# A graph layer on one core: destinations kept on chip and spread by TensorE, float32 queries, another order of loading

## The chip, the cores and the metric

The kernel runs on one core of a Trainium2 chip. The metric is the time of one execution on the device in microseconds (us), less is better; runs are repeated and the median is taken. The engines of the core are named as in the profile: PE (TensorE, matrix products; PEld is its loading of the stationary operand), DVE (VectorE), ACT (ScalarE), POOL (GpSimd, which here mostly issues indirect DMAs) and SP (SyncE, which here issues the plain DMAs). SBUF is the memory on chip with 128 partitions, PSUM the memory that PE writes its results to[...].

## The reference

There are 12500 nodes with 128 features each and 200000 edges, given by `src`, `dst` and `edge_weight`; the edges are sorted by `dst`. For each edge a score is computed from the query of its destination and the key of its source; every destination keeps its 16 best edges, takes a softmax over them, and adds up the messages of the sources. Cut to what matters:

```
h = maximum(layernorm(x), 0)
Qv = h @ W_Q.T ;  Ku = h @ W_K.T
score = sum(Qv[dst] * Ku[src]) / sqrt(128) * exp(-edge_weight)
keep  = rank of the edge among those of its dst, by score, is below 16
alpha = softmax over the kept edges of each dst
agg   = segment_sum(alpha * (h @ W_msg.T)[src], dst)
out   = x + relu(h @ W_self.T + agg)
```

## The kernel before

The edges are cut into chunks of 128, one edge to a partition, and 14 chunks make a group (`GC`); there are 112 groups (`G`). Because a destination's edges can run over the end of a group, a group looks at one chunk more, 15 in all (`NJ`). A group's destinations are at most 128 consecutive nodes, so that node rows also fit on the partitions. W_Q and W_K are multiplied into one matrix beforehand (`a_qk`), so that a query can be multiplied with the raw row `h[src]`.

A first part, the prologue, normalises x and writes h to a table in HBM (`h_tab`); turns the list of sources into columns (`idx_all`, L303 and the helper `to_columns`), and does the same with the destinations (`dst_all`), their places within a node (`pos_all`) and the decay (`dec_all`); and issues the gathers of the first seven groups on POOL, before the loop: the groups below `RAW` = 4 are read from x itself and normalised later (`raw_stats`, `raw_normed`), the others from `h_tab`. A gather (L172) is an indirect DMA of 128 rows of 512 bytes, one chunk; the rows of a group stand in a tile `hs`, of which there are seven.

The main loop (L684) is pipelined in software: iteration i works on different stages of groups i+4 to i-5, and the order of the instructions on each engine is written out by hand; nothing reorders them. In the order of the group's life the stages are:

- `load_nodes` (SP): the group's rows of h and of x. `load_dst` (SP, L186): its 1920 destination numbers, the same on all 128 partitions, 960 KB, into `dstb`.
- `let_go`, called by `more(k)`: DVE copies two columns of `idx_all` into a tile `ix` (L472), and POOL issues two gathers with it. So the place of `more(k)` in DVE's order paces the gathers. `more(0)` and `more(1)` come before `best`, `more(2)` right after it, `more(5)` is the first of the next group and takes a new `hs`.
- `h_turned` (PE L499), `h_turned_out` (ACT L503), `q_made` (PE L506) and `q_out` (ACT L510): the queries of the 128 nodes. `q_parts` (DVE L516) splits each query into three bf16 numbers that add up to it.
- `far_of` (ACT L522): for node p and edge e, the square of dst(e) minus the node's number, from `dstb` and a bias `nb`. `to_edges` (ACT L527): relu(1 - far), which is 1 where they are equal and 0 elsewhere. This is the 0/1 matrix `to_e`, in bf16.
- `q_to_edges` (PE L546), in four blocks of four chunks: the queries put on the edges, the 0/1 matrix times each of the three parts, added up in PSUM, bank "q".
- `scores` (DVE L556): the product with the gathered row, summed over the features, times the decay. `scores_in_slots` (DVE L564), `slots_by_node` (PE L569 and L571), `slots_out` (ACT L576), `node_by_slots` (PE L579): the scores of a node brought beside each other, 40 slots a node, bank "e".
- `best` (DVE L585 to L597): the 16 best of each node. `sum_of_exps` (ACT L602), `one_over_sum` (DVE).
- `kept_to_edges` (PE L614): what a node kept, back on the edges by the 0/1 matrix, bank "x". `on_edges` (DVE L620 to L627), `exps` (ACT L631), `weights` (DVE L635 and L636, into `alz`).
- `sums` (PE L646) in two halves: the weighted sums of the rows of `hs` by node, bank "a". When the second half is done the `hs` is free. `sums_out` (ACT L651), `sums_turned` (PE L654), `sums_turned_out` (ACT L658), `products` (PE L661 and L662), `output` (DVE L666), `store` (SP L672).

Two lines say how the index columns and the broadcast are moved:

```
nc.sync.dma_start(dstb[:, 0:hi - lo], dst[lo:hi].partition_broadcast(P))          # L186
nc.vector.tensor_copy(ix[:, j0:j1], idx_all[:, GC * g + j0:GC * g + j1])          # L472
```

Of the kernel before, what the change touches and what calls it, by code (L numbers as in the profile page):

```python
# [10 lines left out]
F32 = mybir.dt.float32  # L11
BF16 = mybir.dt.bfloat16
I32 = mybir.dt.int32
U32 = mybir.dt.uint32
AF = mybir.ActivationFunctionType
OP = mybir.AluOpType
# [4 lines left out]
P = 128  # L21
# [20 lines left out]
RAW = 4  # L42
# [18 lines left out]
def bc(ap, n):  # L61

    return ap.unsqueeze(2).to_broadcast([ap.shape[0], ap.shape[1], n])


def upper(ap):

    return ap.bitcast(BF16).rearrange("p (n two) -> p n two", two=2)[:, :, 1]


def bm(ap, n):

    return ap.unsqueeze(1).to_broadcast([ap.shape[0], n, ap.shape[1]])
# [3 lines left out]
def gnn_layer(  # L77
# [38 lines left out]
    CPR = 13  # L116
# [4 lines left out]
    assert RR <= P and RR - RF <= 1  # L121
# [10 lines left out]
    def bank(tag, bufs):  # L132
        return psum.tile([P, 512], F32, tag=tag, bufs=bufs, name=tag)
# [10 lines left out]
    nvec = const.tile([P, 1], F32, name="nvec")  # L144
    a_qk = const.tile([P, P], F32, name="a_qk")
# [8 lines left out]
    nb = const.tile([P, G], F32, name="nb")  # L154
# [21 lines left out]
    def gather_at_once(g, table):  # L176
        gather(g, 0, own[g], lambda j: idx_all[:, GC * g + j:GC * g + j + 1], table)

    def load_dst(g):
        n = chunks[g] * P  # L180
        lo = g * EG
        T[g]["dstb"] = dstb = rows_pool.tile([P, NJ * P], I32, name="dstb", bufs=2)
        hi = min(lo + n, M)
        if hi < lo + n:
            nc.vector.memset(dstb[:, hi - lo:n], 1 << 21)
        nc.sync.dma_start(dstb[:, 0:hi - lo], dst[lo:hi].partition_broadcast(P))  # L186
# [47 lines left out]
    with tc.tile_pool(name="edges", bufs=1) as ep, ExitStack() as stage:  # L234
        prep = stage.enter_context(tc.tile_pool(name="prep", bufs=1))
        RL = HALO + RW

        src_r = ep.tile([RR, RL], I32, name="src_r")
        h0 = src_r.bitcast(F32)
        h1 = alz[0][0:RR, 0:RL]  # L240
        dst_all = alz[1][:, 0:CW]
        assert max(RL, CW) <= NJ * (WW + STEP)
        dst_r = ep.tile([RR, HALO + RW], I32, name="dst_r")
# [6 lines left out]
        def load_rows(t, a):  # L250
            if RF:
                nc.scalar.dma_start(t[0:RF, 0:RW], a[0:RF * RW].rearrange("(p c) -> p c", c=RW))
            if REM:
                nc.scalar.dma_start(t[RF:RF + 1, 0:REM], a[RF * RW:M].rearrange("(p c) -> p c", p=1))
# [13 lines left out]
        nc.vector.memset(src_r, 0)  # L268
        load_rows(src_r, src)
        xs, t = [], 0  # L270
        for i, n in enumerate(sizes):
            xg = prep.tile([HP, n, D], F32, name=f"xg{i}")
            for a, b in cuts:
                nc.sync.dma_start(xg[a:b], by_part(x)[a:b, t:t + n, :])
            xs.append((t, n, xg))
            t += n
        make_identity(nc, ident)
        nc.gpsimd.iota(dst_r, pattern=[[1, RL]], base=1 << 21, channel_multiplier=0)
        nc.gpsimd.memset(dst_r[0:1, 0:HALO], -1)
        nc.gpsimd.iota(slots, pattern=[[1, KM]], base=0, channel_multiplier=0,  # L280
# [3 lines left out]
        nc.vector.memset(ew_r, 0.0)  # L284
# [10 lines left out]
        nc.vector.memset(dst_all[:, RR * CPR:CW], float(1 << 21))  # L295
# [13 lines left out]
        def finish(i):  # L309
            t0, n, xg = xs[i]  # L310
            normed(xg, n, *stat[i])
            if i == 1:
                for t, w in zip(ws, (w_q, w_k, w_self, w_msg)):
                    nc.scalar.dma_start(t, w)
                nc.scalar.dma_start(b_i[:, 1:G],
                                    bass.AP(dst.tensor, dst.offset + EG - 1, [[EG, 1], [EG, G - 1]]))

                nc.scalar.dma_start(dst_r[0:1, HALO:], dst[0:RW].rearrange("(p c) -> p c", p=1))
                if RF > 1:
                    nc.scalar.dma_start(dst_r[1:RF, :], bass.AP(dst.tensor, dst.offset + RW - HALO,  # L320
                                                                [[RW, RF - 1], [1, RL]]))
                if REM:
                    nc.scalar.dma_start(dst_r[RF:RF + 1, 0:HALO + REM],
                                        dst[RF * RW - HALO:M].rearrange("(p c) -> p c", p=1))
                load_rows(ew_r, ew)
            for a, b in cuts:
                nc.sync.dma_start(by_part(h_tab)[a:b, t0:t0 + n, :], xg[a:b])
            if i == 1:
                load_dst(0)
# [6 lines left out]
        for g in range(RAW, min(7, G)):  # L336
            gather_at_once(g, h_tab)
# [18 lines left out]
        nc.vector.tensor_copy(row_i[:, 1, G - TAIL:G], row[:, 3, 0:TAIL])  # L356
        pb = bank("s", 1)
# [5 lines left out]
        nc.vector.tensor_copy(dst_f, dst_r)  # L363
        nc.vector.memset(h0[:, 0:1], 0.0)
        nc.vector.tensor_tensor(h0[:, 1:RL], dst_f[:, 1:RL], dst_f[:, 0:RL - 1], op=OP.is_equal)
        nc.vector.tensor_tensor_scan(h1, h0, h0, 0.0, op0=OP.mult, op1=OP.add)
        bb = rows_pool.tile([P, 2, G], F32, name="bb")
        nc.vector.tensor_copy(bb, pb[:, 0:2 * G].rearrange("p (a g) -> p a g", a=2))
        nc.vector.tensor_scalar(nb, bb[:, 0, :], nvec, -1.0, op0=OP.add, op1=OP.mult)
        to_columns(dst_f, HALO, lambda at, p: nc.scalar.copy(at(dst_all), p))  # L370
        to_columns(h1, HALO, lambda at, p: nc.scalar.copy(at(pos_all), p))
        to_columns(ew_r, 0, lambda at, p: nc.scalar.activation(at(dec_all), p, AF.Exp, scale=-1.0))

        byg = dst_all.rearrange("e (g j) -> e g j", j=GC)
        nc.vector.tensor_sub(dlw[:, :, 0:GC], byg[:, 0:G, :], bc(bb[:, 0, :], GC))
        nc.vector.tensor_sub(dlw[:, :, GC], byg[:, 1:G + 1, 0], bb[:, 0, :])
        nc.vector.tensor_tensor(dlw, dlw, bm(w0, G), op=OP.subtract)
        for k in range(2):
            nc.vector.memset(alz[k], 0.0)
# [10 lines left out]
        nc.vector.tensor_copy(badc, bad)  # L390
        t0 = ep.tile([P, TAIL], F32, name="t0")
# [64 lines left out]
    with tc.tile_pool(name="win", bufs=2) as win:  # L456
# [7 lines left out]
        def let_go(g, k):  # L464

            j0, j1 = 2 * k, min(2 * k + 2, own[g])
            if j0 >= j1:
                return
            if k == 0:
                T[g]["ix"] = win.tile([P, GC], I32, name="ix", bufs=4)  # L470
            ix = T[g]["ix"]
            nc.vector.tensor_copy(ix[:, j0:j1], idx_all[:, GC * g + j0:GC * g + j1])  # L472
            gather(g, j0, j1, lambda j: ix[:, j:j + 1])

# [33 lines left out]
        def q_out(g):  # L508
            T[g]["q"] = win.tile([P, 3, D], F32, name="q", bufs=3)
            nc.scalar.copy(T[g]["q"][:, 0, :], so[:, P:2 * P])  # L510

        def q_parts(g):

            q = T[g]["q"]
            for k in range(2):
                nc.vector.tensor_sub(q[:, k + 1, :], q[:, k, :], upper(q[:, k, :]))  # L516


        def far_of(g):
            n = chunks[g] * P  # L520
            T[g]["far"] = win.tile([P, NJ * P], BF16, name="far", bufs=1)
            nc.scalar.activation(T[g]["far"][:, 0:n], T[g]["dstb"][:, 0:n], AF.Square, bias=nb[:, g:g + 1])  # L522

        def to_edges(g):
            n = chunks[g] * P
            T[g]["to_e"] = win.tile([P, NJ * P], BF16, name="to_e", bufs=4)
            nc.scalar.activation(T[g]["to_e"][:, 0:n], T[g]["far"][:, 0:n], AF.Relu, bias=1.0, scale=-1.0)  # L527
# [11 lines left out]
        def q_to_edges(g, b):  # L539
            j0, j1 = 4 * b, min(4 * b + 4, chunks[g])  # L540
            if j0 >= j1:
                return
            T[g]["pq", b] = pq = bank("q", 3)
            for j in range(j0, j1):
                for k in range(3):
                    nc.tensor.matmul(pq[:, (j - j0) * P:(j - j0 + 1) * P],  # L546
                                     lhsT=T[g]["to_e"][:, j * P:(j + 1) * P], rhs=upper(T[g]["q"][:, k, :]),
                                     start=(k == 0), stop=(k == 2))
# [62 lines left out]
        def kept_to_edges(g):  # L611
            T[g]["px"] = px = psum.tile([P, NJ + 1, 64], F32, tag="x", bufs=1, name="x")
            for j in range(chunks[g]):
                nc.tensor.matmul(px[:, j, 0:KM + 3], lhsT=T[g]["to_e"][:, j * P:(j + 1) * P],  # L614
                                 rhs=upper(T[g]["km"]), start=True, stop=True)
# [63 lines left out]
        def at(g, stage, *args):  # L679
            if 0 <= g < G:  # L680
                stage(g, *args)


        for i in range(-3, G + 6):  # L684
            at(i + 3, load_nodes)
            if i + 2 > 0:
                at(i + 2, load_dst)
# [7 lines left out]
            def more(k):  # L695

                g, k = (i + 3, k + 2) if k < 5 else (i + 4, k - 5)
                if 7 <= g < G:
                    let_go(g, k)

            at(i, q_to_edges, 0)
            at(i - 5, output)
# [3 lines left out]
            at(i - 4, sums_turned)  # L706
            at(i - 4, sums_turned_out)
            at(i + 1, q_out)
            at(i, q_to_edges, 1)
            at(i + 1, far_of)  # L710
            at(i - 1, slots_by_node)
            at(i + 1, places)
# [12 lines left out]
            at(i + 1, q_parts)  # L725
# [204 lines left out]
```

## Time and profile before

| | before |
|---|---|
| median of 10 runs | 2691.07 us (2688.03 to 2692.63) |
| profiled execution | 2693.51 us |
| its span, first to last instruction | 2691.7 us |
| granted TensorE clock, mean | 0.694 |
| PE / PEld busy | 1716.5 us (64%) / 1464.7 us (54%) |
| DVE busy | 1475.2 us (55%) |
| POOL busy | 1520.3 us (56%), 1578 instructions |
| ACT busy | 647.9 us (24%) |
| DMA | 253.17 MB, mean 94 GB/s |

How to read it: a profile is one execution. In the lists of groups, a line gives the kernel's line, the engine, the operation, the tiles written and read, their shape and type, and the count; then the busy time in us and the mean of one in ns; then the idle time of the engine just before these instructions and what ended most of it. "remote" is a semaphore whose giver the profile does not name, "issue" is time in which the engine waited for nothing that the profile shows. In the list of waits a line gives engine, tile, line, what it waited for, and then the total in us, how often, and the longest. In the timeline a line gives the start and the duration in us, and in brackets the idle time before. A float32 product has two records of PEld and two of PE, a bf16 product one of each.

### The profile page before, as it was taken

What the parts mean: (1) busy time and instruction counts of PE and PEld (TensorE: products, weight loads), DVE (VectorE), ACT (ScalarE), POOL (GpSimd) and SP (SyncE); (2) the same over time, 40 slices, a digit from 0 to 9 for tenths busy, and PEclk for the clock granted to TensorE, in tenths of its full rate; (3) what the DMA queues carried; (4) which work ended last, traced back from release to release, by engine and by line L of the source; (5) the groups of instructions that cost most, each with busy time, mean ns of one, the idle gap of its engine ahead of it and who ended that gap; (6) DMA issues with size and microseconds to landing.
All of it is one profiled execution on the core that took longest, in us unless ns stands there. A gap on an engine that the chain in (4) does not pass through costs nothing. (4 is left out here: it accounts for less than half of the span.)

```text
span 2691.7 us, 43581 instructions
## 1 busy us (share of the span) xinstructions
PE 1716.5 (64%) x14574; PEld 1464.7 (54%) x14575; DVE 1475.2 (55%) x7420; ACT 647.9 (24%) x1306; POOL 1520.3 (56%) x1578
## 2 busy tenths in 40 slices
PE   0226666766666666666666666666666666766666
PEld 0125555655555555555555555555556555655555
DVE  5446655555555555555555555555555555555555
ACT  5532222222222222222222222222222222222221
POOL 4725555555555555555555555555556555555550
PEclk9667776677677676676666766666676666666778
DMA  8412323232333323322232332322333333222320
GB/s 217 156 57 87 97 92 94 92 94 94 93 95 95 95 94 94 94 90 88 89 93 91 95 94 93 94 94 94 95 95 94 94 93 90 87 90 92 93 80 8
DMA packets 117572, 253.17 MB, mean 94 GB/s; under 512 B 32798, under 2 KB 76065, under 8 KB 116576
## 3 DMA queue, kind: packets, MB, share of 16 engines
q1 hardware_dynamic: 66104, 144.92, 15.6%
q0 software_dynamic: 50144, 102.74, 14.3%
q10 hardware_dynamic: 1094, 2.69, 0.5%
q8 instruction: 115, 1.88, 0.3%
q14 instruction: 115, 0.94, 0.1%
HBM read 236.40 MB, written 14.40 MB: 93 GB/s over the span
## 5 line engine op out<-in xcount | busy, mean ns | idle before, releaser
L172 POOL DMA_INDIRECT hs<-h_tab,ix x1465 | 1410.6, 963 | 1044.0 <-DVE prod L556 493.7
L546 PE MATMUL q<-q,to_e 128*128 128x128 bf16 x5022 | 553.8, 260 | 316.1 <-issue 261.8
L646 PE MATMUL a<-hs,alz 128*128 128x128 f32 x3348 | 694.3, 373 | 92.3 <-issue 81.0
L646 PEld LDWEIGHTS a<-hs,alz 128*128 128x128 f32 x3348 | 636.7, 279 | 140.4 <-issue 119.7
L546 PEld LDWEIGHTS <-to_e 128*128 128x128 bf16 x5022 | 421.8, 116 | 396.5 <-issue 384.6
L556 DVE SCALAR_TENSOR_TENSOR prod<-hs,dec_all,q 128x128 f32<-128x128 f32 x1674 | 483.0, 342 | 75.5 <-remote 35.4
L585 DVE TENSOR_SCALAR ell<-slots,e 128x40 f32<-128x40 f32 x112 | 28.0, 250 | 869.8 <-remote 811.2
L571 PE MATMUL e<-ow,sl 128*41 128x40 f32 x3348 | 251.2, 251 | 44.0 <-issue 42.1
L602 ACT ACTIVATE e<-v,km 128x16 f32<-128x16 f32 x112 | 34.4, 307 | 976.8 <-DVE km L594 959.7
L571 PEld LDWEIGHTS e<-ow,sl 128*41 128x41 f32 x3348 | 221.3, 166 | 68.7 <-issue 54.3
L654 PE MATMUL s<-ident,agn 128*128 128x128 f32 x112 | 41.2, 368 | 301.7 <-ACT up L631 153.9
L651 ACT ACTIVATE agn<-a,rden 128x128 f32<-128x128 f32 x112 | 41.1, 367 | 766.4 <-remote 515.2
L522 ACT ACTIVATE far<-dstb,nb 128x1920 bf16<-128x1920 int32 x112 | 213.0, 1902 | 0.0
L527 ACT ACTIVATE to_e<-far 128x1920 bf16<-128x1920 bf16 x112 | 201.1, 1796 | 0.0
L654 PEld LDWEIGHTS s<-ident,agn 128*128 128x128 f32 x112 | 17.7, 158 | 326.1 <-ACT up L631 172.2
L556 DVE DVE_READ_ACCUMULATOR prod<-hs,dec_all,q 128x1 f32 x1674 | 136.1, 81 | 0.0
L472 DVE COPY ix<-idx_all 128x2 int32<-128x2 int32 (+1 forms) x733 | 130.2, 178 | 0.0
L614 PE MATMUL x<-km,to_e 128*128 128x43 bf16 x1674 | 81.1, 203 | 42.8 <-DVE km L597 21.4
L614 PEld LDWEIGHTS <-to_e 128*128 128x128 bf16 x1674 | 67.9, 111 | 68.2 <-DVE km L597 44.0
L666 DVE SCALAR_TENSOR_TENSOR o<-s,x_t 128x128 f32<-128x128 f32 x112 | 32.5, 290 | 128.8 <-issue 119.3
L506 PE MATMUL s<-a_qk,hT 128*128 128x128 f32 x224 | 56.9, 337 | 64.5 <-ACT hT L503 55.9
L564 DVE TENSOR_TENSOR sl<-po,s 128x600 f32<-128x600 f32 x112 | 87.5, 782 | 4.4 <-DVE prod L556 0.6
(166 smaller groups left out, 1634.8 us busy)
## 6 DMA issues: line engine op xcount, KB each, us to landing
dstb<-in_dst_dram SPq DMA_DIRECT2D x111, 960.0 KB
hs<-h_tab,ix POOLq DMA_INDIRECT x1465
h_r<-h_tab SPq DMA_DIRECT2D x112, 64.0 KB
x_t<-in_x_dram SPq DMA_DIRECT2D x108, 64.0 KB
out_dram<-o SPq DMA_DIRECT2D x108, 64.0 KB
xg<-in_x_dram SPq DMA_DIRECT2D x2, 1400.0 KB
h_tab<-xg SPq DMA_DIRECT2D x2, 1400.0 KB
xg<-in_x_dram SPq DMA_DIRECT2D x1, 1120.0 KB
```

The costliest lines, as they stand in the source:

```text
L172: nc.gpsimd.indirect_dma_start(out=T[g]["hs"][:, j, :], out_offset=None, in_=table[0:N, :], in_offset=bass.IndirectOffsetOnAxis(ap=index(j ...
L472: nc.vector.tensor_copy(ix[:, j0:j1], idx_all[:, GC * g + j0:GC * g + j1])
L506: nc.tensor.matmul(so[:, P:2 * P], lhsT=T[g]["hT"], rhs=a_qk, start=True, stop=True)
L522: nc.scalar.activation(T[g]["far"][:, 0:n], T[g]["dstb"][:, 0:n], AF.Square, bias=nb[:, g:g + 1])
L527: nc.scalar.activation(T[g]["to_e"][:, 0:n], T[g]["far"][:, 0:n], AF.Relu, bias=1.0, scale=-1.0)
L546: nc.tensor.matmul(pq[:, (j - j0) * P:(j - j0 + 1) * P], lhsT=T[g]["to_e"][:, j * P:(j + 1) * P], rhs=upper(T[g]["q"][:, k, :]), start=(k ...
L556: nc.vector.scalar_tensor_tensor(prod, rows_of(g, j), dec_all[:, c:c + 1], T[g]["pq", b][:, (j % 4) * P:(j % 4 + 1) * P], op0=OP.mult, op1 ...
L564: nc.vector.tensor_tensor(sl1[g % 2][:, 0:n, 0:KM], T[g]["po"][:, 0:n, :], bc(T[g]["s"][:, 0:n], KM), op=OP.mult)
L571: nc.tensor.matmul(et[0:KM + 1, STEP * j:STEP * j + WN], lhsT=sl1[g % 2][:, j, :], rhs=T[g]["ow"][:, j, :], start=False, stop=(j == n - 1))
L614: nc.tensor.matmul(px[:, j, 0:KM + 3], lhsT=T[g]["to_e"][:, j * P:(j + 1) * P], rhs=upper(T[g]["km"]), start=True, stop=True)
L646: nc.tensor.matmul(T[g]["pa"][:, 0:P], lhsT=alz[g % 2][:, WW * j + PRE:WW * j + PRE + P], rhs=rows_of(g, j), start=(j == 0), stop=(j == n ...
L654: nc.tensor.transpose(so[:, 2 * P:3 * P], T[g]["agn"], ident)
```

## The change

The destination numbers are no longer loaded once more for each group as a broadcast. The rows of `dst_r`, which the prologue loads anyway, are kept on chip as `rel`, one group to a row: destination minus the number of the group's first node, in bf16, 1920 to a row. For group g, PE multiplies one column of the identity matrix, repeated 128 times, with `rel`, which puts row g on all partitions, in four pieces of up to 512 columns in PSUM. ACT squares each piece with the node's own number as a bias. The pieces use bank "a", which has one buffer and also holds the sums; a piece can be written when ACT has read the one before. Their places in the order of the loop are shown in the diff.

The 0/1 matrix is in float32 and so is q; `q_parts` is gone and `q_to_edges` has one float32 product for a chunk in place of three bf16 ones. `kept_to_edges` reads the upper halves of the float32 numbers as a strided bf16 operand.

In the prologue all loads are issued by SP, the sources first, where ACT issued some of them before. `RAW` is 3: 42 gathers are issued at once from x. The gathers of group 3 go through `let_go` between steps of the prologue on DVE, those of groups 4, 5 and 6 are issued in the iterations -1, 0 and 1 of the loop. A row of the prologue's tiles is now a whole group (`CPR` = `GC`), `dlw` is made from `rel` with matrix products, and the memset of `alz` is done by POOL.

```diff
-RAW = 4
+RAW = 3
...
-    CPR = 13
+    CPR = GC
...
+    rel = const.tile([RR, RW + P], BF16, name="rel")
...
-    def load_dst(g):
-        n = chunks[g] * P
-        lo = g * EG
-        T[g]["dstb"] = dstb = rows_pool.tile([P, NJ * P], I32, name="dstb", bufs=2)
...
-        nc.sync.dma_start(dstb[:, 0:hi - lo], dst[lo:hi].partition_broadcast(P))
+    def let_go(g, k):
+
+        j0, j1 = 2 * k, min(2 * k + 2, own[g])
+        if j0 >= j1:
+            return
+        if k == 0:
+            T[g]["ix"] = rows_pool.tile([P, GC], I32, name="ix", bufs=6)
+        ix = T[g]["ix"]
+        nc.vector.tensor_copy(ix[:, j0:j1], idx_all[:, GC * g + j0:GC * g + j1])
+        gather(g, j0, j1, lambda j: ix[:, j:j + 1])
...
-                nc.scalar.dma_start(t[0:RF, 0:RW], a[0:RF * RW].rearrange("(p c) -> p c", c=RW))
+            nc.sync.dma_start(t[0:RF, 0:RW], a[0:RF * RW].rearrange("(p c) -> p c", c=RW))
...
+        for k in range(2):
+            nc.gpsimd.memset(alz[k], 0.0)
...
-        for g in range(RAW, min(7, G)):
-            gather_at_once(g, h_tab)
...
+        let_go(RAW, 0)
...
+        nc.vector.tensor_scalar(rel, dst_f[:, HALO:], dst_f[:, HALO - 1:HALO], 1.0, op0=OP.subtract, op1=OP.subtract)
+        let_go(RAW, 2)
...
-            T[g]["q"] = win.tile([P, 3, D], F32, name="q", bufs=3)
-            nc.scalar.copy(T[g]["q"][:, 0, :], so[:, P:2 * P])
-
-        def q_parts(g):
-
-            q = T[g]["q"]
-            for k in range(2):
-                nc.vector.tensor_sub(q[:, k + 1, :], q[:, k, :], upper(q[:, k, :]))
-
-
-        def far_of(g):
-            n = chunks[g] * P
-            T[g]["far"] = win.tile([P, NJ * P], BF16, name="far", bufs=1)
-            nc.scalar.activation(T[g]["far"][:, 0:n], T[g]["dstb"][:, 0:n], AF.Square, bias=nb[:, g:g + 1])
+            T[g]["q"] = win.tile([P, D], F32, name="q", bufs=3)
+            nc.scalar.copy(T[g]["q"], so[:, P:2 * P])
+
+
+        def far_of(g, b):
+            n0, n1 = 4 * P * b, min(4 * P * (b + 1), chunks[g] * P)
+            if n0 >= n1:
+                return
+            if b == 0:
+                T[g]["far"] = win.tile([P, NJ * P], BF16, name="far")
+            pr = bank("a", 1)
+            nc.tensor.matmul(pr[:, 0:n1 - n0], lhsT=upper(ident[0:RR, g:g + 1]).to_broadcast([RR, P]),
+                             rhs=rel[:, n0:n1], start=True, stop=True)
+            nc.scalar.activation(T[g]["far"][:, n0:n1], pr[:, 0:n1 - n0], AF.Square, bias=minus)
...
-            T[g]["to_e"] = win.tile([P, NJ * P], BF16, name="to_e", bufs=4)
+            T[g]["to_e"] = win.tile([P, NJ * P], F32, name="to_e", bufs=4)
...
-                for k in range(3):
-                    nc.tensor.matmul(pq[:, (j - j0) * P:(j - j0 + 1) * P],
-                                     lhsT=T[g]["to_e"][:, j * P:(j + 1) * P], rhs=upper(T[g]["q"][:, k, :]),
-                                     start=(k == 0), stop=(k == 2))
+                nc.tensor.matmul(pq[:, (j - j0) * P:(j - j0 + 1) * P],
+                                 lhsT=T[g]["to_e"][:, j * P:(j + 1) * P], rhs=T[g]["q"], start=True, stop=True)
...
-                nc.tensor.matmul(px[:, j, 0:KM + 3], lhsT=T[g]["to_e"][:, j * P:(j + 1) * P],
+                nc.tensor.matmul(px[:, j, 0:KM + 3], lhsT=upper(T[g]["to_e"][:, j * P:(j + 1) * P]),
...
-            if i + 2 > 0:
-                at(i + 2, load_dst)
...
-                g, k = (i + 3, k + 2) if k < 5 else (i + 4, k - 5)
-                if 7 <= g < G:
+                if i in (-1, 0, 1):
+                    g = i + 5
+                else:
+                    g, k = (i + 3, k + 2) if k < 5 else (i + 4, k - 5)
+                    if g < 7:
+                        return
+                if i >= -1 and g < G:
                     let_go(g, k)
 
             at(i, q_to_edges, 0)
+            at(i + 1, far_of, 0)
             at(i - 5, output)
             at(i - 5, store)
             at(i - 3, weights)
             more(0)
             at(i - 4, sums_turned)
+            at(i + 1, far_of, 1)
             at(i - 4, sums_turned_out)
             at(i + 1, q_out)
             at(i, q_to_edges, 1)
-            at(i + 1, far_of)
+            at(i + 1, far_of, 2)
             at(i - 1, slots_by_node)
+            at(i + 1, far_of, 3)
             at(i + 1, places)
...
-            at(i + 1, q_parts)
```

## The prediction, made before the changed kernel ran

> **What bounds the kernel now.** I read the groups first, then the waits of 1000 to 2000 us, then the timeline of single cycles. The chain of what ended last covers only the last microseconds and says nothing of the loop. In the groups the reader should compare counts with idle time:
>
> ```profile
> L172 POOL DMA_INDIRECT hs<-h_tab,ix x1465 | 1410.6, 963 | 1044.0 <-DVE prod L556 493.7
> L546 PE MATMUL q<-q,to_e 128*128 128x128 bf16 x5022 | 553.8, 260 | 316.1 <-issue 261.8
> L646 PE MATMUL a<-hs,alz 128*128 128x128 f32 x3348 | 694.3, 373 | 92.3 <-issue 81.0
> ...
> L585 DVE TENSOR_SCALAR ell<-slots,e 128x40 f32<-128x40 f32 x112 | 28.0, 250 | 869.8 <-remote 811.2
> ...
> L522 ACT ACTIVATE far<-dstb,nb 128x1920 bf16<-128x1920 int32 x112 | 213.0, 1902 | 0.0
> ...
> dstb<-in_dst_dram SPq DMA_DIRECT2D x111, 960.0 KB
> ```
>
> No engine is full. POOL issues 1465 gathers in the loop, each 0.96 us busy and about 0.30 us of issue: 14 x 1.25 = 17.5 us a group. The loop from the first of them (215.4 us) to the last (2614.5) takes 2399 us for 105 groups, 22.85 us each, so about 5.3 us per cycle is POOL waiting. The waits say for what:
>
> ```profile
> DVE ell L585 <- remote: 353.6, 41, 8.7
> ...
> POOL hs L172 <- DVE prod L556: 187.6, 86, 4.3
> ```
>
> DVE stands 8.7 us a cycle before `best` (L585), and POOL once up to 4.3 us behind DVE, because the next index copy (L472) is queued behind `best`. One cycle in time:
>
> ```profile
> 1552.74 0.29 PE L571 MATMUL e<-ow,sl 128*41 128x40 f32 x3 [0.19 <-issue]
> ...
> 1555.60 0.99 PE L546 MATMUL q<-q,to_e 128*128 128x128 bf16 x5 [0.49 <-issue]
> ...
> 1557.33 0.94 POOL L172 DMA_INDIRECT hs<-h_tab,ix  x1 [0.30 <-issue]
> ...
> 1560.03 0.25 DVE L585 TENSOR_SCALAR ell<-slots,e 128x40 f32<-128x40 f32 x1 [8.74 <-remote]
> ...
> 1562.42 0.94 POOL L172 DMA_INDIRECT hs<-h_tab,ix  x1 [4.15 <-DVE prod L556]
> ```
>
> L585 waits for the last L571. PE's record of it ends at 1553.03, yet DVE starts 7 us later, 1.76 us after the last gather was issued (1558.27), when its packets had landed. Meanwhile PE makes a pass or a handful, waits 0.5 us for nothing the profile shows ("issue"), and goes on. **While gathers stream, PE crawls and what it has done reaches the others late.** Two more places support this. In the last iterations, without gathers, the same wait is nothing:
>
> ```profile
> 2624.79 0.25 DVE L585 TENSOR_SCALAR ell<-slots,e 128x40 f32<-128x40 f32 x1 [0.35 <-PE e L571]
> ```
>
> Those iterations last 12.5 to 14.3 us, though they too read a broadcast `dstb`. And in the prologue, where POOL issues gathers without a pause until 160.9 us, PE hardly moves from 118 on and then stands:
>
> ```profile
> 169.25 0.79 PE L506 MATMUL s<-a_qk,hT 128*128 128x128 f32 x2 [45.61 <-ACT hT L503]
> ```
>
> So a cycle is: eight gathers (10.0 us), a gap of 4.1 (drain 1.8, `best` 2.0, copy and issue 0.4), six gathers (7.5), a gap of 1.7 until the sums of L646 give an `hs` buffer back. Sum 23.3 less the 0.3 issue counted at each gap: 22.7, against 22.85.
>
> **Part by part, for one group in the loop.**
>
> *The 960 KB broadcast goes.* 111 x 960 KB is 43% of the 253 MB moved. No instruction waits for it in the listing of 1000 to 2000 us, L522 has 0.0 us idle before it, and SP only issues it. Its removal frees nothing on the path. Two bounds: if the broadcast slows the gathers' landing, the 1.8 us of drain could fall to 1 us (-0.8); but in the packets it holds the gathers back some 2 to 3 us at each cycle's start, in which PE works at its normal rate (L571's 27 passes in 1.81 us from 1550.74). Without it the crawl begins earlier: up to the 30 passes of L571, 1.4 us hot and 2.1 cold, move behind the drain (+1.4 to +2.1). I take the second, since the stall follows gathers in every stretch above.
>
> *Four products and four reads of PSUM replace L522.* Before: one ACT instruction of 1.90 us, from SBUF. After: for each of four pieces, PE (at most 512 columns, four bf16 passes' worth of 0.070, 0.28 us, twice that at half the clock) and ACT's Square. The nearest ACT row is the prologue's read of 128x484 from PSUM: four in 2.90 us, 0.73 each. So ACT 2.9 instead of 1.9 us (+1.0, ACT is busy 24%: hidden), PE +1.1 to +2.2. The new thing is the chain: all pieces use the one buffer of bank "a", so each product waits for ACT to have read the piece before, and the sums (L646), which share it, wait for the last. By the program's order pieces 0, 1 and 2 stand on PE ahead of L571; piece 3 stands behind it and ahead of q's third block, the transposition L499 and the first half of the sums. Queued behind a waiting piece is therefore all PE work of `best`, and behind that DVE's index copies, POOL's next six gathers.
> A hop from PE to ACT costs 0.96 us when the stream has not started (L654 1548.85, aggT 1549.81). Inside it the trace has one:
>
> ```profile
> 1643.54 0.45 PE L654 MATMUL s<-ident,agn 128*128 128x128 f32 x1 [6.54 <-issue]
> ...
> 1648.08 0.27 ACT L658 COPY aggT<-s 128x128 f32<-128x128 f32 x1 [10.97 <-remote]
> ```
>
> That is 4.5 us. Three hops of 1 us would fit into the ten of the burst (bound +0); if one of them ends only with the drain, piece 2 (0.3 to 0.5) and the passes of L571 (1.4 to 2.1) come after it, where now only 0.4 us does. Together with the lost lull, the same passes are late, once: **+1.8 us**, the range 0 to 2.5.
>
> *q in float32, one product.* Before 3 x 15 bf16 passes: 12 take 0.84 us hot, 0.070 each, 3.15 us. After 2 x 15 passes such as L646's, 16 in 2.00, 0.125 each: 3.75. The Trainium skill (FP8 and Floating Point Precision, TensorE Precision Notes) says that true FP32 takes four passes: 15 x 4 x 0.070 = 4.2 us, +1.05, which speaks against the change; the row has two longer records and +0.6. I take the row. Most lies beside DVE's scores; what falls between `best` and the release of `hs` counts, with piece 3 and its read ahead of the sums: block 2 and piece 3 add 0.2 + 0.4 + 0.75 = 1.3 us there, of which `best` itself (2.0 us on DVE) covers most: **+0.4 us** (0 to 1.3). If that cover is gone the scatter to the edges (L614) falls into the second burst, which is the second rival below. DVE loses L516, 2 x 0.3 = 0.6 us a group; it stands behind the index copies on DVE and DVE waits 8.7 us a cycle: nothing.
>
> *L614 reads every second bf16 of the float32 matrix.* No row shows a strided load; L614's 15 loads take 0.54 us, twice that would be +0.5, less than nothing is excluded since the count is the same. I take 0, keeping 0.5.
>
> *The prologue.* 42 gathers are issued from x at once, then those of group 3 between DVE steps and 14 in each of the windows -1, 0, 1; POOL issues the same 1563 in all. Before, POOL stands from 160.9 to 215.4 us, and the loop that started at 94 stood for the 98 gathers. After, group 3 can follow `h_tab` (about 108 us), three windows at a loop's pace with gathers, 22 us, end at 175, and two windows without (12.5 to 14) bring group 7 at about 200 or a little earlier. The memset of `alz` goes from DVE to POOL before the gathers. All loads on SP's queue, the sources ahead, can bring the first gather (24 us) forward by some us; the x loads and `h_tab` stores queued behind them on SP may lose as much. **-20 us**, between 0 and -40 (all of the stand but one window).
>
> *Sum.* 105 x (1.8 + 0.4) = +231; -20; profiled execution 2693.5, so 2904. The median of the runs shown is 2.4 below that execution: about **2900**.
>
> **Rivals.**
> *A, the cycle stays, only the prologue gains.* For it: the cycle is 22.8 to 22.9 us at a granted clock of 0.5 as at 1.0, so PE's own length doesn't show; the three hops fit if each takes 1 us. Against: the 4.5 us hop. 2691 - 20 = 2671, between 2650 and 2690.
> *B, the stall shrinks.* If it is DMA traffic as such, 43% less of it takes drain and part of the crawl away: cycle 21 us, 105 x -1.85 - 20 gives 2477, up to 2600. Against: iterations with `dstb` but no gathers show no stall.
> *C, both gaps grow.* In one cycle of before (1456.7 to 1484.5) L614 slipped into the second burst: `on_edges` came late, the second gap was 6.3 us instead of 1.7, the cycle 27.6. If piece 3 and the longer products do this each time: 105 x 4.75 - 20 = +479, 3170; half the cycles, 2930.
> *D, slower only by the prologue:* sources and nodes behind one queue, nothing in the loop: 2700 to 2715.
>
> **How the numbers follow.** Forecast, 2780 to 3030, 0.42. C above that, 0.17. A 0.21, B 0.15, D and no change 0.05. Faster by over 0.2% (about what a measurement here tells from no change) is A and B, 0.36; within it 0.03; slower 0.61. The range reaches from B's upper part to C's time, 2560 to 3180; the forecast's own is 2780 to 3030.
>
> **What would show it.** Right: the gap on POOL before the six gathers is 5.5 to 6.5 us and ends with L585's successor, the index copy; L571's counterpart lies after the burst; ACT's pieces of `far` are spread over the burst, one at least over 3 us behind its product; the iterations at the end without gathers are 13 to 16 us. Wrong: pieces following each other at 1 us inside the burst (A), the wait of `best` ending while gathers flow, or gathers closer than 1.25 us (B); a second gap over 4 us (C). The sum fails altogether if the crawl was due to the broadcast after all, or if the bursts are cut into other lengths than eight and six.

## The result, and the profile after

| | before | after |
|---|---|---|
| median | 2691.03 us (31 runs, 2683.88 to 2696.47) | 2660.69 us (9 runs, 2646.53 to 2667.04) |
| ratio | | 0.9884, interval 0.9871 to 0.9896 |
| span of the profiled execution | 2691.7 us | 2658.9 us |
| 99th gather (the first of group 7) | 215.4 us | 207.0 us |
| from there to the last gather | 2399.1 us | 2373.5 us |
| last gather to the end | 77.1 us | 78.4 us |
| DMA | 253.17 MB | 143.40 MB |
| granted TensorE clock, mean | 0.694 | 0.777 |

The change made the kernel 1.2% faster where 8% slower was forecast. The difference of the spans, 32.8 us, is 8.4 us before the loop's gathers and 25.6 us within them, less 1.3 us behind them. One thing must be known to read the rest: in the sets of runs below the kernel before took 2691, 2715 to 2717 or, in one set, 2081 us, so every ratio is to runs of the kernel before in the same set, on the same chip.

The groups of the page of the changed kernel that answer to those shown of before:

```profile
L174 POOL DMA_INDIRECT hs<-h_tab,ix x1521 | 1478.3, 972 | 1027.2 <-DVE prod L545 377.5
L635 PE MATMUL a<-hs,alz 128*128 128x128 f32 x3348 | 577.3, 341 | 443.9 <-ACT far L513 351.8
...
L536 PE MATMUL q<-q,to_e 128*128 128x128 f32 x3348 | 617.5, 332 | 84.7 <-issue 76.8
...
L513 ACT ACTIVATE far<-a,minus 128x512 bf16<-128x512 f32 (+1 forms) x447 | 294.9, 660 | 942.0 <-remote 648.8
...
L574 DVE TENSOR_SCALAR ell<-slots,e 128x40 f32<-128x40 f32 x112 | 28.1, 251 | 798.6 <-remote 756.6
```

And its waits of 1000 to 2000 us:

```profile
DVE ell L574 <- remote: 317.5, 41, 8.6
ACT far L513 <- remote: 263.1, 41, 7.3
...
PE a L635 <- ACT far L513: 161.2, 35, 5.6
POOL hs L174 <- DVE prod L545: 142.8, 42, 4.0
```

The picture of before is still there: `best` (now L574) waits 7.7 us each time it waits (317.5 in 41), POOL behind it. The new waits that the prediction spoke of are there too: ACT's piece waits 6.4 us each time, and the sums (L635) 4.6 us for ACT. Yet the cycle didn't grow. One cycle shows why:

```profile
1503.89 0.94 POOL L174 DMA_INDIRECT hs<-h_tab,ix  x1 [1.81 <-PE q L536]
...
1505.27 0.38 PE L511 MATMUL a<-rel,ident 112*128 112x512 bf16 x1 [0.66 <-ACT far L513]
...
1505.68 0.69 ACT L513 ACTIVATE far<-a,minus 128x512 bf16<-128x512 f32 x1 [0.47 <-issue]
...
1506.76 0.63 PE L511 MATMUL a<-rel,ident 112*128 112x512 bf16 x1
...
1507.43 0.69 ACT L513 ACTIVATE far<-a,minus 128x512 bf16<-128x512 f32 x1 [0.74 <-PE a L511]
1507.57 2.14 PE L560 MATMUL e<-ow,sl 128*41 128x40 f32 x30
...
1509.64 0.34 PE L511 MATMUL a<-rel,ident 112*128 112x384 bf16 x1
...
1509.81 1.05 PE L536 MATMUL q<-q,to_e 128*128 128x128 f32 x8
...
1512.83 0.94 POOL L174 DMA_INDIRECT hs<-h_tab,ix  x1 [0.31 <-issue]
...
1515.39 0.25 DVE L574 TENSOR_SCALAR ell<-slots,e 128x40 f32<-128x40 f32 x1 [8.60 <-remote]
1515.42 0.58 ACT L513 ACTIVATE far<-a,minus 128x384 bf16<-128x384 f32 x1 [7.30 <-remote]
...
1516.06 3.27 PE L635 MATMUL a<-hs,alz 128*128 128x128 f32 x14 [5.08 <-ACT far L513]
...
1519.03 0.94 POOL L174 DMA_INDIRECT hs<-h_tab,ix  x1 [0.30 <-issue]
```

The burst's first gather was issued at 1503.89. The three pieces that stand ahead of L560 hop to ACT in 0.4 to 0.7 us (medians of the loop 0.41, 0.62, 0.67 from the product's start), in time for L560 to be on record at 1509.71. Only piece 3, which stands behind L560, is stuck: its product is recorded at 1509.64, ACT reads it at 1515.42 (median 5.0 us). DVE is let go within 0.03 us of ACT, 1.6 us after the last gather's instruction ended. So in this cycle the wait for the end of the burst hides PE's additional work, and piece 3's wait ends with the one that was there before.

The semaphore events of the trace, which aren't complete, show what is late. PE raises one counter with the last product of L560, with piece 3, with L536 and with L490, which start at 1509.50, 1509.64, 1510.59 and 1510.70. The four rises are recorded together, between 1515.36 and 1515.52, and DVE starts 0.03 us after the first of them. Whether PE's results were ready much earlier isn't shown: the ends of its records are modelled.

Between the groups the distance of one `best` to the next is 22.85 us by the median, in both kernels. But 26 of 97 cycles of the changed kernel take about 21.5 us or less, against 2 of before; in those `best` starts 0.9 us after the eighth gather's issue instead of 2.5, and the ninth gather is issued 3.3 us after the eighth instead of 4.9 (medians).

### The profile page after: what moved, and what is told of

Its sections match the earlier page's. It is cut to its first block, busy times and chain, and to the rows that moved or that the text cites. A ratio compares the mean times of both kernels' runs of the same rounds, so it can differ in the third digit from the quotient of the medians.

```text
span 2658.9 us, 40952 instructions
## 1 busy us (share of the span) xinstructions
PE 1748.8 (66%) x13352; PEld 1509.2 (57%) x13353; DVE 1430.5 (54%) x7198; ACT 721.5 (27%) x1622; POOL 1529.2 (58%) x1580
## 2 busy tenths in 40 slices
DMA packets 101392, 143.40 MB, mean 54 GB/s; under 512 B 30988, under 2 KB 74252, under 8 KB 100405
## 5 line engine op out<-in xcount | busy, mean ns | idle before, releaser
L635 PE MATMUL a<-hs,alz 128*128 128x128 f32 x3348 | 577.3, 341 | 443.9 <-ACT far L513 351.8
L635 PEld LDWEIGHTS a<-hs,alz 128*128 128x128 f32 x3348 | 539.2, 251 | 474.7 <-ACT far L513 370.1
L536 PE MATMUL q<-q,to_e 128*128 128x128 f32 x3348 | 617.5, 332 | 84.7 <-issue 76.8
L536 PEld LDWEIGHTS q<-q,to_e 128*128 128x128 f32 x3348 | 565.0, 241 | 187.2 <-issue 166.2
L513 ACT ACTIVATE far<-a,minus 128x512 bf16<-128x512 f32 (+1 forms) x447 | 294.9, 660 | 942.0 <-remote 648.8
L574 DVE TENSOR_SCALAR ell<-slots,e 128x40 f32<-128x40 f32 x112 | 28.1, 251 | 798.6 <-remote 756.6
L511 PE MATMUL a<-rel,ident 112*128 112x512 bf16 (+1 forms) x447 | 220.0, 492 | 192.8 <-ACT agn L640 120.7
L560 PE MATMUL e<-ow,sl 128*41 128x40 f32 x3348 | 212.0, 243 | 0.6 <-DVE sl L553 0.6
L560 PEld LDWEIGHTS e<-ow,sl 128*41 128x41 f32 x3348 | 198.0, 159 | 14.5 <-DVE sl L553 0.7
L518 ACT ACTIVATE to_e<-far 128x1920 f32<-128x1920 bf16 x112 | 201.2, 1796 | 0.0
L189 DVE COPY ix<-idx_all 128x2 int32<-128x2 int32 x761 | 151.0, 199 | 0.0
L625 DVE TENSOR_TENSOR alz<-ow,kept 128x600 f32<-128x600 f32 x112 | 87.9, 785 | 4.0
L603 PEld LDWEIGHTS <-to_e 128*128 128x128 bf16 x1674 | 79.9, 114 | 12.4 <-issue 4.4
```

The source lines that it names most:

```text
L511: nc.tensor.matmul(pr[:, 0:n1 - n0], lhsT=upper(ident[0:RR, g:g + 1]).to_broadcast([RR, P]), rhs=rel[:, n0:n1], start=True, stop=True)
L513: nc.scalar.activation(T[g]["far"][:, n0:n1], pr[:, 0:n1 - n0], AF.Square, bias=minus)
L536: nc.tensor.matmul(pq[:, (j - j0) * P:(j - j0 + 1) * P], lhsT=T[g]["to_e"][:, j * P:(j + 1) * P], rhs=T[g]["q"], start=True, stop=True)
L560: nc.tensor.matmul(et[0:KM + 1, STEP * j:STEP * j + WN], lhsT=sl1[g % 2][:, j, :], rhs=T[g]["ow"][:, j, :], start=False, stop=(j == n - 1))
L625: nc.vector.tensor_tensor(alz[g % 2].rearrange("e (j w) -> e j w", w=WW + STEP)[:, 0:n, 0:WN], T[g]["ow"][:, 0:n, :], bc(kept[:, 0:n], WN) ...
L635: nc.tensor.matmul(T[g]["pa"][:, 0:P], lhsT=alz[g % 2][:, WW * j + PRE:WW * j + PRE + P], rhs=rows_of(g, j), start=(j == 0), stop=(j == n ...
```

## The experiments

**Is it the stream of gathers?** In the changed kernel the loop's gathers, from group 7 on, become plain loads of the same size; they bring other rows, so the sums are wrong.

```diff
-        gather(g, j0, j1, lambda j: ix[:, j:j + 1])
...
+        for j in range(j0, j1):
+            nc.sync.dma_start(T[g]["hs"][:, j, :], h_tab[P * j:P * (j + 1), :])
```

> The changed kernel with the loop's gathers from group 7 on replaced by plain loads of 128 consecutive rows of h_tab each, on SP's queue: the same bytes in the same tiles, the sums are of wrong rows. If the stream of indirect gathers is what holds the loop (PE's results seen only when it pauses, POOL's 17.5 us a group), the loop goes at the pace of the last iterations, 12.5 to 14.5 us a group, total 1700 to 1950 us, and the wait at best is under 1 us. If PE, ACT and their waits bound it, 20 us or more a group, over 2400.

Measured, in one run: 1666 us, beside 2691 of before. The page shows DVE and PE working as the bound:

```profile
PE 1301.8 (78%) x13352; PEld 1155.4 (69%) x13353; DVE 1385.4 (83%) x7198; ACT 727.3 (44%) x1622; POOL 106.5 (6%) x115
```

So PE, ACT and DVE can do the whole list in 1666 us with those 143 MB moved; the indirect gathers add about 1000 us to the changed kernel. Of these some 420 are there in the set of 2081 us too, where the changed kernel takes 2087 and POOL's own pace is the cycle (below); the other 570 or so come only where the loop stalls.

**Is the broadcast's traffic worth anything?** It was taken from the kernel before, where later groups then read the tiles of the first two and match their edges with wrong nodes, the work being the same; and it was added to the changed kernel, unread.

The kernel before (e5):

```diff
     def load_dst(g):
+        if g >= 2:
+            T[g]["dstb"] = T[g % 2]["dstb"]
+            return
```

The changed kernel (e1, e1b, e1c), with `load_dst` writing a tile of half the size twice:

```diff
             at(i + 3, load_nodes)
+            if i + 2 > 0:
+                at(i + 2, load_dst)
```

> The kernel before with the broadcast loaded for the first two groups only; later groups read those two tiles, so the edges are matched with wrong nodes, the work otherwise being the same. Theory T (traffic): the loop falls from 2399 to about 2373 us, some cycles of 21.5 us appear, total about 2665. Theory P: no change, 2691. The prediction's own argument (the broadcast shields PE from the gathers, so that without it the passes of L571 come after the drain): the cycle grows by 1 to 2 us, total 2790 to 2900.

> The changed kernel, to which the 960 KB broadcasts of every group are added again, written to a tile that nothing reads. Theory T (the loop got 26 us shorter because the broadcast's packets are gone): the loop from the 99th gather to the last goes back from 2373 to about 2399 us, nearly all cycles are 22.85 us again, those of 21.5 us vanish; the total is 2680 to 2690. Theory P (it got shorter because PE has other products, not because of traffic): the loop stays within 6 us of 2373, total 2655 to 2668.

> The changed kernel itself, since the first four runs stood beside a kernel before of 2715 us, not 2691. If what the change gives is the same on such a chip, its ratio is 0.988 again and e1 to e3 (1.003, 1.008, 1.008) each show a real loss. If the gain hangs on how long the gathers take there (a cycle of 22.85 us against some 23.2), the ratio is about 1.000 to 1.005, the short cycles of 21.5 us are missing, and e1 shows that the traffic is worth nothing.

> The changed kernel with the broadcasts added again, unread. If the traffic takes part in the stall: slower than the control by over 0.4%, and the cycles of 21.5 us are rarer. If not: within 0.2% of the control.

> The changed kernel as the control of the next three. 0.989 where the kernel before takes 2691 us, about 1.003 where it takes 2081.

Measured: e5 0.9998 (0.9989 to 1.0007). e1 1.0028 (1.0017 to 1.0038) in a set where before took 2715 us; it had no control, and c1 ran in another (before 2691) and gave 0.9891 (0.9876 to 0.9906). The pair that counts is e1c, 1.0018 (1.0004 to 1.0031), beside its control c3, 1.0010 (0.9997 to 1.0024), before 2717: no difference. 43% of the bytes are worth nothing, as the first half of the prediction's step said; its second half, that the broadcast shields PE and that 1.4 to 2.1 us come in its place, fell with e5.

c3 says something else too: in the set of 2717 us the changed kernel isn't faster at all. In c3 95 of the 97 cycles take 23.0 to 23.3 us and one is short. e1 and e5, both in the set of 2715 us, show where it goes: the changed kernel with the broadcasts (e1) is 13.3 us earlier at its 99th gather than the kernel before without them (e5), and its loop is 15.0 us longer (2433.9 against 2418.9), where in the first two profiles it was 25.6 us shorter. The size of the gain hangs on the occasion; why 26 cycles were short in the first profile, 12 in c1's and one here stays open. The granted clock isn't it: it is 0.78 in c3 as in the first profile of the changed kernel.

**What is the float32 form worth?** Alone in the kernel before (e4), and undone in the changed one (e2). In e13 before has two of the three bf16 products, with the subtractions left in.

The edit of e4 is the one of the change itself (`to_e` and `q` in float32, `q_parts` gone), e2 is its reverse; e13:

```diff
-                for k in range(3):
+                for k in range(2):
...
-                                     start=(k == 0), stop=(k == 2))
+                                     start=(k == 0), stop=(k == 1))
```

> The kernel before with the float32 0/1 matrix and one float32 product a chunk (the broadcast kept; x_t and hT have one buffer less to make room). The prediction's sum: 0.4 us a cycle more, ratio 1.016. Theory P (the float32 form helps, as e2 against e1 and the changed kernel suggests): ratio 0.99 to 0.997. Theory H (all that PE does in the stream of gathers is hidden by the wait for its end): 1.000.

> The changed kernel with the 0/1 matrix in bf16 again, q in three bf16 parts and three products a chunk (the two subtractions of q on DVE too). Theory T (traffic): the loop stays at about 2373 us, total 2655 to 2668, since the product's form lies beside the stream of gathers. Theory P (the float32 products are what shortened the loop): loop about 2399, total about 2687.

> The kernel before with two of the three bf16 products of a chunk: the lowest part of q is left out of the scores. All else stays, the subtractions on DVE too. If the float32 form gained by PE's shorter list (60 records for a group's products in place of 90): 0.990 to 0.994, as in e4. If it gained by the DVE operations that went: 1.000.

Measured: e4 0.9915 (0.9902 to 0.9929), where the whole change gave 0.9891. e2 1.0076 (1.0062 to 1.0090), against 1.0028 of e1 in its own set (with the broadcasts, which are worth nothing) and 1.0010 of c3 in a like one. So where the loop stalls the float32 form is worth 0.5 to 0.9%, some 14 to 22 us, and was forecast to cost 42. In the loop itself it is 16.6 us from before to e4, and 5.5 from e2 to e1. e13 gives 0.9940 (0.9917 to 0.9963): a shorter list of products on PE is enough for 0.6%, with DVE's subtractions still there, and at a lower granted clock (0.67 against 0.70 of before; e4 has 0.79), so a higher clock isn't what it takes. A group's products are 60 records of PE and PEld in float32, 60 in e13, 90 before; that the number of records is what counts, rather than the time of the third pass, isn't separated.

**What is the new plan of the first gathers worth?** In the changed kernel groups 3 to 6 are issued at once again, as before.

```diff
+        for g in range(RAW, min(7, G)):
+            gather_at_once(g, h_tab)
...
-        let_go(RAW, 0)
...
-                if i in (-1, 0, 1):
-                    g = i + 5
```

> The changed kernel with the gathers of groups 3 to 6 issued at once ahead of the loop again, as before the change, and no gathers in the iterations -1, 0 and 1. If the new plan of the first gathers is worth the 8.4 us by which the 99th gather came earlier (207.0 against 215.4), the 99th gather comes at 214 to 217 us and the total is 8 us more, about 2669. If the gain came from the loads ahead of it instead (the sources first on SP), the 99th gather stays at 205 to 209 us and the total at 2661.

Measured: 1.0082 (1.0066 to 1.0097), 0.5% above e1 of its own set and 0.7% above c3, so 15 to 20 us. The 99th gather comes at 224.6 us; in e1 it comes at 204.9. The plan is worth about what was forecast, -20. In the same set the 99th gather of e5, which has the prologue of before, comes at 218.2. So the rest of the new prologue, without the plan, costs 6.4 us; which part of it isn't separated. And the two iterations without gathers were reckoned too short: POOL stands idle for 31.7 us before the 99th gather of the changed kernel (175.4 to 207.0), where 25 to 28 were reckoned.

**Is the gap before the ninth gather in the wrong place?** Two edits of the changed kernel: the index copies ahead of `best` (e8), and `best` itself at the head of the iteration, ahead of `slots_by_node`, so that it waits for the transposition of the iteration before (e10, e10c).

e8:

```diff
             more(1)
+            more(2)
             at(i - 2, best)
-            more(2)
```

e10 and e10c:

```diff
+            at(i - 2, best)
             more(0)
...
             more(1)
-            at(i - 2, best)
             more(2)
```

> The changed kernel with the index copies of more(2) moved ahead of best on DVE, so that POOL's ninth and tenth gather do not wait for best. If the results of PE are seen only when the gathers pause, best itself is now 2.5 us later and the pause comes after the tenth: the cycle keeps its length (within 1%). If POOL's wait of 4 us were only a matter of DVE's order, the cycle gets 2 to 3.5 us shorter, total 2300 to 2450.

> The changed kernel with best, on DVE, ahead of the first two index copies of an iteration, and ahead of slots_by_node in the program, so that it waits for the transposition at the end of the iteration before and no longer for the passes of L560, which wait for it instead. Theory W (the gap before the ninth gather is only a wait in the wrong place): the gap goes, POOL issues 14 gathers with one gap, the cycle is 18.5 to 20 us, total 2230 to 2400. Theory H (PE's results come through only when the gathers pause, so that a pause of some length is needed in each cycle): the time lost at that gap comes back at the other, the cycle is 22 to 24 us, total 2600 to 2760.

> The changed kernel with best ahead of the index copies and of slots_by_node. Where the loop stalls. Theory W (the gap before the ninth gather is a wait in the wrong place): cycle 18.5 to 20 us, 2230 to 2400. Theory H (a pause of the gathers is needed for PE's results, wherever it falls): cycle 22 to 24 us, 2600 to 2760.

Measured: e8 0.9925 (0.9910 to 0.9940), its control c1 0.9891; the cycle keeps its length (mean 22.9 us beside 22.8), the gaps only move. e10 0.9886 (0.9870 to 0.9901) in the set of 2081 us, below its control of 1.0025. And e10c **1.1541** (1.1511 to 1.1571) in one of 2717: with 14 gathers in one stream, `best` no longer waits, but everything else does:

```profile
1517.91 0.34 PE L511 MATMUL a<-rel,ident 112*128 112x384 bf16 x1
...
1528.94 0.95 POOL L174 DMA_INDIRECT hs<-h_tab,ix  x1 [0.30 <-issue]
...
1532.34 0.58 ACT L513 ACTIVATE far<-a,minus 128x384 bf16<-128x384 f32 x1 [15.10 <-remote]
```

Piece 3 now takes 14.4 us to reach ACT, until 2.4 us after the last gather's instruction ended, and the cycle is 27.5 us. The wait isn't in the wrong place: where the loop stalls, a pause is what lets PE's results through.

**Is the pause as long as it need be?** e15 puts the two index copies inside `best`, behind its second search; e14 behind its first, with the scatter to the edges ahead of the sums on PE.

In both, `more(2)` is handed to `best` as `between`. e14:

```diff
             nc.vector.max(v16[:, 0:8], ell)
+            between()
...
+            at(i - 2, kept_to_edges)
             at(i - 3, sums, 0)
-            at(i - 2, kept_to_edges)
```

e15:

```diff
             nc.vector.max(v16[:, 8:16], rest)
+            between()
```

> The changed kernel with the two index copies of more(2) inside best, behind its first search of the eight largest, and with the scatter to the edges (L603) ahead of the first half of the sums on PE. If the cycle is gathers plus pauses: the first pause is 1.4 us shorter, 105 x 1.4 = 147 us, so 0.94 to 0.96 of the kernel before where that takes 2691 to 2717 us, and no change beside the changed kernel where it takes 2081. If PE's work needs the whole pause: L603 falls into the stream, the second gap grows to 4 us or more, ratio 1.03 to 1.15.

> The changed kernel with the same copies behind the second search of best, nothing else moved. If the cycle is gathers plus pauses: 0.7 us less, 105 x 0.7 = 74 us, ratio 0.96 to 0.975 where the kernel before takes 2691 to 2717. If PE's work needs the whole pause: 1.00 to 1.05.

Measured, before 2717 us: e14 **0.9578** (0.9554 to 0.9602), 2603 us, the fastest of all where the loop stalls; e15 1.0449 (1.0420 to 1.0478). e15 is the changed kernel with the copies moved and nothing else. e14 has two edits, and what each is worth wasn't tried alone. The timelines show where e15 loses. e14:

```profile
1507.42 0.25 DVE L574 TENSOR_SCALAR ell<-slots,e 128x40 f32<-128x40 f32 x1 [7.74 <-remote]
...
1508.47 0.94 POOL L174 DMA_INDIRECT hs<-h_tab,ix  x1 [2.55 <-DVE rest L580]
...
1509.52 0.73 PE L604 MATMUL x<-km,to_e 128*128 128x43 bf16 x15 [7.35 <-DVE km L587]
...
1513.12 0.20 DVE L610 TENSOR_REDUCE up<-x 128x15 f32<-128x45 f32 x1
```

and e15:

```profile
1514.81 0.94 POOL L174 DMA_INDIRECT hs<-h_tab,ix  x1 [3.25 <-DVE rest L582]
...
1516.37 0.76 PE L604 MATMUL x<-km,to_e 128*128 128x43 bf16 x15
...
1522.01 0.20 DVE L610 TENSOR_REDUCE up<-x 128x15 f32<-128x45 f32 x1 [3.07 <-PE s L497]
...
1524.96 0.94 POOL L174 DMA_INDIRECT hs<-h_tab,ix  x1 [2.97 <-PE a L511]
```

After a pause the first packets move 1.65 us after the gather is issued (the median, in before and after alike). In e14 the scatter (L604) ends at 1510.25, 1.78 us after the ninth gather was issued at 1508.47, and DVE goes on with it as soon as it is free. In e15 the scatter stands behind the sums, which piece 3 has held up; it starts 1.56 us after the gather and ends 2.32 us after it. DVE then waits 3.07 us (the record names L497, PE's latest work; L610 reads what L604 wrote), and the median distance from the sixth gather of the second burst to the next group's first is 5.3 us instead of 3.0.

Over all cycles of the traces this distance goes with the end of the scatter. Where the scatter ends up to 2.3 us after the ninth gather's issue, the distance is 2.8 to 3.0 us by the median (after, c3, e14); where it ends later, 3.8 in after (15 cycles) and 5.3 in e15 (96). So the scatter may end some 0.6 us after the first packets move, but not much more. The changed kernel itself stands close to this: its scatter ends 2.2 us after the gather by the median.

In e14 the distance from the eighth gather to the ninth is 3.5 us, 1.35 less than in c3, the cycle 21.98 instead of 23.22: the sum of gathers and pauses holds, as long as the scatter comes in time.

**Where nothing stalls.** In one set the kernel before took 2081 us, and three runs meant as a control and its pairs stood there:

> The changed kernel once more, as the control on the chip on which the next two run. About 0.989 where the kernel before takes 2691 us.

> The changed kernel with the broadcasts added again, unread, now beside a control. Theory T (the broadcast's traffic is part of what the change gained): slower than the control by 0.6% or more, most cycles 22.85 us again. If traffic is worth nothing: within 0.2% of the control.

> The changed kernel with the bf16 matrix and three products, beside a control. The kernel before with the float32 form alone was 0.9915, so undoing it should cost 0.8% or more: ratio 0.996 to 1.002. If the float32 form only paid together with the broadcast, this is within 0.2% of the control.

Measured: 1.0025 (1.0013 to 1.0036), 1.0020 (1.0008 to 1.0032) and 1.0021 (1.0012 to 1.0030): the change itself costs 0.25% there, and neither undoing the float32 form nor adding the broadcasts makes a difference. The same program's waits end by themselves there, in the stream:

```profile
1204.31 0.34 PE L511 MATMUL a<-rel,ident 112*128 112x384 bf16 x1
...
1204.41 0.25 DVE L574 TENSOR_SCALAR ell<-slots,e 128x40 f32<-128x40 f32 x1 [2.49 <-PE e L560]
...
1204.68 0.58 ACT L513 ACTIVATE far<-a,minus 128x384 bf16<-128x384 f32 x1 [1.41 <-PE a L511]
1204.73 0.95 POOL L174 DMA_INDIRECT hs<-h_tab,ix  x1 [0.30 <-issue]
```

Piece 3 reaches ACT in 0.38 us with gathers on both sides. The cycle is 17.7 us, POOL's 14 x 1.25 and little else.

## Why the prediction was wrong

*What bounds the kernel* was right where it stalls: gathers plus pauses (e6, e14), and PE's results late until the stream ends (e10c). "While gathers stream, PE crawls" was half of it. In the changed kernel PE records L560 and four products of L536 (eight records) at their usual pace inside the stream; what is late is the counter that tells ACT and DVE.

*The broadcast goes: nothing on the path* was right (e5, e1c). The lost lull, +1.4 to +2.1 us, was wrong, and the packets were misread. In the cycle that the prediction shows SP issues the load only here:

```profile
1552.06 0.34 SPq L186 DMA_DIRECT2D dstb<-in_dst_dram  x1
```

Its packets move from about 1553.5 to 1556.5, behind the passes of L571 (1550.74 to 1553.03) and not beside them, and PE crawls in just that time. There was no lull for L571 to lose.

*The step that failed* is the price of the four pieces: "if one of them ends only with the drain", piece 2 and the passes of L571 come after it, **+1.8 us**. The bound +0 was named, and the slow hop of 4.5 us taken instead. That hop was an exception: its product was itself 6.5 us late, and of the 100 hops from L654 to L658 in the loop of before two take over 1.5 us, with a median of 0.98. The three pieces ahead of L560 take 0.4 to 0.7 us each and are through some 3.5 us after the burst's first gather, before anything is held up; piece 3 does end with the drain, but behind L560, so `best` doesn't wait for it. What the pieces cost shows e2, which has them without the float32 form: its loop took 2439 us, e5's in the same set, which has neither, 2419. That is 0.2 us a cycle where +1.8 was forecast. The last iterations without gathers, forecast at 13 to 16 us, take 14.0, 12.5 and 13.2, as before (12.6, 14.3 and 12.5).

*The float32 product, +0.4 us*, had the wrong sign: in the loop -0.16 us a cycle from before to e4, -0.05 from e2 to e1. The sum counted the time of the passes, and that did grow as the row said, by 0.6 us a group (553.8 to 617.5 us busy), but the loop didn't get longer by it. The measured gain came with a shorter list for PE, in e13 as well; why a shorter list helps stays open.

*The prologue, -20*, was right for the plan itself (19.7 us from e3 to e1 at the 99th gather); the rest of the new prologue takes part of it back, and 8.4 us were left in the first profile.

*Rival A*, the cycle stays and only the prologue gains, gave 2671 and was nearest: the median cycle is 22.85 us before and after. That its number fits is luck in part: it put 20 us into the prologue, where 8.4 were found, and nothing into the loop, where the short cycles make the gain of the first profile and are missing in c3. One of its reasons was misread as well: no stretch at a clock of 1.0 in the loop of before lasts over 10.3 us, so no cycle ran at 1.0; the cycles' means are 0.57 to 0.80, and within these the cycle doesn't change. *Rival C's* mechanism, the scatter slipping into the second burst, wasn't set off by the change, but e15 shows it: 4.5%. Half of the cycles would have made 2920 in its sum, not 2930.

## What to carry to other kernels

A wait that ends at an outside moment, here the end of a burst of gathers, hides most of what is put ahead of it; before an added chain is priced, ask for each link whether it comes before that moment anyway, and take the usual hop for it, not the rare one. Where a stream must pause for the other engines, work through the pause item by item: what must be inside (here the scatter, by some 2.3 us after the next gather's issue) and what merely stands there (the end of `best`). With both edits (e14) this gave 4.2%; moving the copies alone (e15) cost 4.5%, and moving `best` (e10c) 15%.

## What the runs showed of the hardware that was not expected

The same kernel took 2691, 2715 to 2717 or 2081 us, steadily within a set (24 runs from 2077.53 to 2084.66 in one). The gathers were issued 1.25 us apart each time, 32 packets to a gather each time; what differed is how soon PE's counter rises while gathers stream: piece 3 of the same program reaches ACT in 0.38 us at 2081 and in 5.0 us at 2661. Not the whole stream holds it up: the pieces of the first 3.5 us of a burst hop in 0.4 to 0.7 us. In e10c too the rises come in a bunch: those of four instructions that start between 1517.77 and 1523.82 are recorded between 1532.28 and 1532.44. The change gave 1.1 to 1.2% in the sets of 2691 us, nothing in the one of 2717, and cost 0.25% in the one of 2081. What decides it wasn't found; sets of 2715 and of 2081 us bore the same chip number, so the chip may not be it. Inside a burst POOL's idle time before a gather stays at 0.30 us, so no hop from DVE to POOL was seen held up; whether bytes, descriptors or the number of packets hold the counter up wasn't tried. And an order that is best where the loop stalls needn't be where it doesn't: e10 is 1.4% better than its control in one case and 15% worse in the other.
